# A deformable convolution beside a recurrence: partial sums in a PSUM bank, turned tiles and states in another, tile by tile

## The chip, the cores and the metric

The kernel runs on one core of a Trainium2 chip. The metric is the device time of one execution in microseconds (us). The kernel before took 3271.92 us, the median of three runs (3266.55 to 3273.73).

A core has a tensor engine (PE in the profile; PEld is its loading of weights), a vector engine (VectorE, DVE), a scalar engine (ScalarE, ACT), GpSimd (POOL) and a queue engine for transfers (SyncE, SP). SBUF is the working memory, and PSUM the memory that PE writes its results to. The kernel uses PSUM as eight banks of 128 partitions by 512 fp32 numbers.

## What is computed

The input is `x`, 4 images of 256 channels and 64 by 64 places, all in fp32. There are two layers. Cut to what matters:

```
# layer 0
x = x + deformable_conv(norm_over_channels(x))   # 9 taps, each sampled at 4 corners
t = tokens(x)
t = t + lstm(norm_over_channels(t))              # recurrence over the tokens
# layer 1
x = x + gate(x) * norm_over_channels(x)          # a gate per image and channel, from mean, max, std
t = tokens(x)
t = t + lstm(norm_over_channels(t))
```

The deformable convolution first computes, for each place and tap, an offset and a mask from the normalized input. The sample of a tap is `mask` times the bilinear mean of four corners, `w0*c0 + w1*c1 + w2*c2 + w3*c3`, each corner a vector of 256 channels. The sum over taps of samples times a 256x256 matrix is the output:

```
val = (1-wy)*(1-wx)*corner(y0,x0) + (1-wy)*wx*corner(y0,x1)
    + wy*(1-wx)*corner(y1,x0) + wy*wx*corner(y1,x1)
out = einsum('bkhwc,ock->bohw', val * mask, w_conv)
```

The step of the recurrence has three weighted gates with inputs `x @ U + h @ V + b`, and its cell is not the usual one, `c_new = h * c + i * g`, `h_new = o * tanh(c_new)`.

## The kernel before

**Tiles.** The 16384 places are 128 tiles of 128 places by 256 channels (`NTILE` is 128, `P` 128, `C` 256). A tile holds the same column position of all images, and one time step of the recurrence works on one tile. The order of tiles (`ORDER`) has 16 warm-up tiles ahead of the 128, so that there are 144 steps (`STEPS`).

**Stages.** `prepare` computes offsets and weights and writes the normalized input to a table in DRAM. `sample_and_recur` samples, convolves and runs the first recurrence side by side. `Gate` collects and then forms the gate of the second layer, and `gated_lstm` runs the second recurrence. The change touches `sample_and_recur` and the helper class `Spare`.

**Rounds.** Two units (a tile and a tap) make a round; there are 576 (`PAIRS`). For a round `n`, `gather` (L621) has POOL fetch four corners for each unit into `squares`; `scale` (L642) has ScalarE write `v = w0 * c0`; `combine` (L649) has VectorE add the other three corners with scalar_tensor_tensor, q outer and the two units inner; `turn` (L655) has PE transpose the two `v` into a PSUM bank `tr`; `copy` (L662) has ScalarE bring it to SBUF as `vt`; `convolve` (L669) has PE multiply it with the tap's matrix and add in `acc`. When a pair of tiles has all nine taps, `sampled` (L737) adds the input (`plus`, L711), stores the pair, and asks for the sums of squares (`spread`, L716), which ask for the norms (`norms`, L750, in the parts `begin`, `second`, `last`).

**The path to the recurrence.** `normed` (L832) has ScalarE write normalized tiles `xn`, two at a time; `turned` (L843) has PE make four transposes of them into one PSUM bank, `xt`; `kept` (L854) has ScalarE copy the bank to SBUF as `cm`. `project_part` (L937) multiplies a tile of `cm` with the input weights into the gates' banks `ga` and `gb`, `recur` (L497) adds the state's part, and `core` (L982) places these and the gates at fixed slots: a step is 4.5 slots (`step_slot`, L920), and a slot is a round while there are samples.

**The path from the recurrence.** `added` (L960) has PE transpose a step's state `h` into a PSUM bank `ht`, and VectorE adds it to the tile (`add` inside it, with `plus`). The tile's second norm follows, and then `styled` (L860): ScalarE writes the tile normalized and squared as `y`, VectorE adds it to `lanes` and takes the maximum into `gmx` (`lanes`, `highest`). These feed the gate of the second layer.

**Spare time.** What has no fixed slot is given to `Spare` (L548) for an engine, with a slot from which it may go, an estimate in microseconds and a condition (`room`), such as a free buffer. At each slot, `fill` (L1042) runs what fits in the estimate of the slot's remaining time, from the front of the engine's list; `urgent` puts an item at the front, everything else goes to the end.

**The order of instructions.** All engines run their instructions in the order in which the program gives them (`Ordered`, `InOrder`), one slot after the other: ACT's part, then VectorE's, PE's, and the gathers. The waits between engines follow from which tiles an instruction reads and writes.

**PSUM.** The eight banks are `tr` (2), `acc` (2), `ga`, `gb`, and two of the pool `misc`, with the tags `ms` and `ys`. In `sample_and_recur`, `ht` uses `ms` and `xt` uses `ys`. After the sampling the gate's sums (`Gate.add`, tile `pq`) take `ys`, and `Gate.gates` takes `ms`.

Of the kernel before, what the change touches and what calls it, by code (L numbers as in the profile page):

```python
# [11 lines left out]
F32 = mybir.dt.float32  # L12
I32 = mybir.dt.int32
AF = mybir.ActivationFunctionType
ALU = mybir.AluOpType
# [4 lines left out]
P = 128  # L20
B, C, H, W = 4, 256, 64, 64
T = H * W
NC = C // P
# [13 lines left out]
NB = 8  # L37
# [510 lines left out]
class Spare:  # L548
# [3 lines left out]
    def __init__(self):  # L552
        self.todo = {}

    def give(self, engine, slot, us, do, room=lambda: True, urgent=False):
        left = self.todo.setdefault(engine, [])
        left.insert(0 if urgent else len(left), (slot, us, do, room))

    def run(self, engine, slot, us, late=6):
        left = self.todo.get(engine, [])  # L560
        n = 0
        while n < len(left):
            ready, cost, do, room = left[n]
            if ready <= slot and room() and (cost <= us + 0.3 or slot - ready > late):
                del left[n]
                us -= cost
                do(slot)
                n = 0
            else:
                n += 1  # L570
# [5 lines left out]
def sample_and_recur(  # L576
# [12 lines left out]
    nc = Ordered(tc.nc, pools["after"])  # L589
    ident = const[0]  # L590
# [8 lines left out]
    give = spare.give  # L599
# [5 lines left out]
    LAST = STEPS - NB  # L605
# [36 lines left out]
    def scale(n):  # L642
        r = rounds[n]
        for i in range(2):
            v = vp.tile([P, C], F32, name="v", tag="v", bufs=6)
            nc.scalar.activation(v, r["sq"][i][:, 0:C], AF.Copy, scale=r["w"][i][0])
            r["v"].append(v)

    def combine(n):  # L649
        r = rounds[n]  # L650
        for q in range(1, 4):
            for v, sq, w in zip(r["v"], r["sq"], r["w"]):
                nc.vector.scalar_tensor_tensor(v, sq[:, q * C : (q + 1) * C], w[q], v, ALU.mult, ALU.add)

    def turn(n):  # L655
        r = rounds[n]
# [59 lines left out]
    def spread(n, k, b, j, slot):  # L716

        su, nm, ss = stat(b)
        nc.scalar.activation(nm[:, j : j + k], su[:, j : j + k], AF.Copy, scale=-1.0 / C)
        for i in range(k):  # L720
            c = slice(j + i, j + i + 1)
            sq = sm.tile([P, C], F32, name="sq", tag="sqb", bufs=1)
            nc.scalar.activation(sq, place(n + i)[:, 0], AF.Square, bias=nm[:, c], accum_out=ss[:, c])

        left[b].update(range(j, j + k))
        if b < NTILE // NB:
            parts = (0, NB // 2, 2 * NB if b >= 4 else NB)
        else:
            parts = range(NB, 2 * NB + 1, {STEPS // NB + 1: 2, STEPS // NB: 4}.get(b, NB))
        for lo, hi in zip(parts, parts[1:]):  # L730
            if j in range(lo, hi) and left[b] >= {*range(lo, hi)}:
                norms(b, lo, hi, slot + (2 if LAST <= n < STEPS - 1 else 1))

    left = {b: set() for b in range(STEPS // NB + 2)}
    factors = {}

    def sampled(p, slot):  # L737
        x, a = place(2 * p, 2), acc.pop(p)
        b, j = divmod(2 * p, NB)
        for i in range(2):  # L740
            plus(x[:, i], a[:, i], b, j + i)
        nc.sync.dma_start(x1[:, ORDER[2 * p] : ORDER[2 * p] + 2], x)
        give("ACT", slot + 1, 1.5, lambda s: spread(2 * p, 2, b, j, s))

    eps = sm.tile([P, 2 * NB], F32, name="epsb", tag="epsb", bufs=1)
    nc.vector.memset(eps[:, 0:NB], 1e-5)
# [3 lines left out]
    def norms(b, lo, hi, slot):  # L750


        _, nm, ss = stat(b)
        if b not in factors:
            keep = ("rs", "low") if b < WARM // NB else ()
            factors[b] = [
                sm.tile(
                    [P, 2 * NB], F32, name=n, tag=f"{n}b{b}" if n in keep else f"{n}b", bufs=1 if n in keep else 3
                )
                for n in ("d", "v", "rs", "low")  # L760
            ]
        d, v, rs, low = (f[:, lo:hi] for f in factors[b])
        if hi > NB:
            first = max(lo - NB, 0)
            mine = slice(ORDER[(b - 2) * NB] + first, ORDER[(b - 2) * NB] + hi - NB)
        if lo >= NB:
            rs, low = gate.rs[:, mine], gate.low[:, mine]

        def newton():
            nc.vector.tensor_mul(d, rs, rs)  # L770
            nc.vector.scalar_tensor_tensor(d, d, -0.5, v, ALU.mult, ALU.mult)
            nc.vector.scalar_tensor_tensor(rs, d, 1.5, rs, ALU.add, ALU.mult)

        def begin(slot):
            nc.vector.scalar_tensor_tensor(v, ss[:, lo:hi], 1.0 / C, eps[:, lo:hi], ALU.mult, ALU.add)
            nc.vector.tensor_scalar(
                rs.bitcast(I32), v.bitcast(I32), -0.5, float(0x5F3759DF), ALU.mult, ALU.add
            )
            newton()
            if n0 >= LAST:  # L780
                second(slot)
            else:
                give("DVE", slot, 0.9, second)

        def second(slot):
            newton()
            newton()
            if n0 >= LAST:
                last(slot)
            else:  # L790
                give("DVE", slot, 0.4, last)

        def last(slot):
            nc.vector.tensor_mul(low, nm[:, lo:hi], rs)
            if b < WARM // NB:
                normal[b] = factors[b][2:]
            if lo < NB:
                for p in range(max(lo, FIRST if b == 0 else 0) // 2, min(hi, NB) // 2):
                    give(
                        "ACT",  # L800
                        slot + 1 + 7 * (p - lo // 2),
                        0.9,
                        lambda s, p=p: normed(b, p, *factors[b][2:], s),
                        room("xn", 2),
                    )
            if hi > NB:
                if lo < NB:
                    nc.vector.tensor_copy(gate.rs[:, mine], rs[:, NB + first - lo :])
                    nc.vector.tensor_copy(gate.low[:, mine], low[:, NB + first - lo :])
                if n0 == STEPS - 2:  # L810
                    ending(slot)
                    return
                for p in range(first // 2, (hi - NB) // 2):
                    give(
                        "ACT",
                        slot + 2 + 3 * (p - first // 2),
                        1.15,
                        lambda s, p=p: styled(b - 2, p, s),
                        room("y", 2),
                    )  # L820

        n0 = (b - 2) * NB + lo - NB
        give("DVE", slot, 0.9 if n0 < LAST else 2.2, begin, urgent=n0 >= LAST)


    now, free = {"slot": 0}, [*range(SQUARES)]
    taken = {"xn": 0, "y": 0, "ms": 0, "ys": 0, "cm": 0}

    def room(tag, n):
        return lambda: free if tag == "y" and now["slot"] > PAIRS + 16 else taken[tag] < n  # L830

    def normed(b, p, rs, low, slot):  # L832

        taken["xn"] += 1
        xn = yp.tile([P, 2, C], F32, name="xn", tag="xn")
        n = b * NB + 2 * p
        for i in range(2):
            normalize(nc, xn[:, i], place(n + i)[:, 0], rs, low, 2 * p + i)
        if n < WARM:
            through.update((n, n + 1))  # L840
        give("PE", slot + 1, 0.44, lambda s: turned(n, xn, s), room("ys", 1))

    def turned(n, xn, slot):  # L843
        taken["ys"] += 1
        pt = ps_ms.tile([P, 2, NC, P], F32, name="xt", tag="ys")
        for i in range(2):
            for k in range(NC):
                nc.tensor.transpose(pt[:, i, k], xn[:, i, k * P : (k + 1) * P], ident)
        taken["xn"] -= 1
        give("ACT", slot + 1, 0.6, lambda s: kept(n, pt), room("cm", 6))  # L850

    cms = {}

    def kept(n, pt):  # L854
        taken["cm"] += 1
        cms[n] = cm_p.tile([P, 2, NC, P], F32, name="cm", tag="cm")
        nc.scalar.copy(cms[n], pt)
        taken["ys"] -= 1

    def styled(b, p, slot):  # L860

# [98 lines left out]
    def added(n, slot):  # L960

        h = state.pop(("h", n))
        taken["ms"] += 1
        ht = ps_ms.tile([P, C], F32, name="ht", tag="ms")
        for k in range(NC):
            nc.tensor.transpose(ht[:, k * P : (k + 1) * P], h[:, k], ident)

        def add(slot):
            b, j = divmod(n, NB)
            plus(place(n)[:, 0], ht, b + 2, NB + j)  # L970
            taken["ms"] -= 1
            if j == NB - 1:
                t0 = ORDER[n] - NB + 1
                nc.sync.dma_start(x2[:, t0 : t0 + NB], place(b * NB, NB))
            if n >= LAST:
                spread(n, 1, b + 2, NB + j, slot)
            else:
                give("ACT", slot + 1, 0.9, lambda s: spread(n, 1, b + 2, NB + j, s))

        give("DVE", slot + 1, 0.48, add, urgent=n >= LAST)  # L980
# [79 lines left out]
    s = 0  # L1060
# [865 lines left out]
```

## Time and profile before

| what | value |
|---|---|
| median of three runs | 3271.92 us |
| lowest and highest | 3266.55 and 3273.73 us |
| span of the profiled execution | 3304.8 us |
| first and last gather issued (POOL) | 192.5 and 2304.0 us |
| samples beside the recurrence, full | about 420 to 2300 us |
| first recurrence alone | about 2320 to 2480 us |
| gate and second recurrence | about 2480 to 3305 us |
| sample additions (`v<-squares,used,v`, VectorE) | 3456 of 128x256, mean 477 ns |
| transposes of tiles (`xt`, PE) | 328, copied by 82 of 128x512 (mean 579 ns) |
| transposes of states (`ht`, PE) | 272, read by 128 additions of 128x256 (mean 414 ns) |

Times in the profile are those of one execution, recorded by the hardware; it was some 1% longer than the median of the runs. An instruction's duration runs from its start to its end. Successive instructions of VectorE can overlap, so that the busy time of a group (a union) is less than count times mean. Nearly all instructions carry the line L425, that of the helper that records the order, so that rows are told apart by the names of the tiles: `out<-in`. In group rows, the numbers are: instructions, busy time, mean duration, idle time of the engine just ahead of them, and what ended that idle time. In rows by stage, after the stretch and its length come the busy times of PE, PEld, DVE, ACT and POOL with instruction counts, then the granted clock of PE as a share, the share of DMA engines busy, and GB/s. Timeline rows have a start, a length, and the instructions merged in it; in brackets is the engine's idle time before them and who ended it.

### The profile page before, as it was taken

The page shows a single profiled execution, that of the slowest core. Times are in us where ns is not written, and L with a number is a line of the kernel's source. Part 1 is how long each engine was busy: PE and PEld are TensorE (multiplying, and loading weights), DVE is VectorE, ACT ScalarE, POOL GpSimd, SP SyncE. Part 2 cuts the span into 40 slices and gives each one's busy share as a digit, 9 for nine tenths or more (in the row PEclk, how much of TensorE's full clock was granted, in tenths as well). Part 3 has the DMA queues.
Part 4 walks back from the last instruction along what each step waited for, and adds up shares of the span by engine and source line. Part 5 has one row for each costly group of instructions (what it writes and reads, how often), then busy time and mean ns, then how long its engine had stood idle before and what let it go on. Part 6 is the DMA issues. An engine that isn't in the chain of part 4 may idle for free.

```text
span 3304.8 us, 61570 instructions
## 1 busy us (share of the span) xinstructions
PE 3072.2 (93%) x20428; PEld 2841.5 (86%) x20428; DVE 2621.7 (79%) x7465; ACT 2059.5 (62%) x5450; POOL 1629.7 (49%) x1595
## 2 busy tenths in 40 slices
PE   7957799999999999999999999999896999999998
PEld 6945688898899989898888888989894999999997
DVE  6666677888898988898889888979567777777774
ACT  6724455566666666676666666757775666666663
POOL 3366666665566666675757656656000022222221
PEclk9978899999999999999999999999997999999999
DMA  9988787898989989888889988888101044444442
GB/s 314 326 292 322 292 280 285 297 321 300 329 298 336 326 295 333 308 310 312 301 309 328 317 295 309 312 311 304 62 14 71 26 138 153 148 151 153 147 141 85
DMA packets 311432, 822.38 MB, mean 249 GB/s; under 512 B 100024, under 2 KB 105528, under 8 KB 306496
## 3 DMA queue, kind: packets, MB, share of 16 engines
q0 software_dynamic: 189312, 672.57, 58.6%
q1 hardware_dynamic: 121360, 145.15, 12.9%
q8 instruction: 164, 2.69, 0.3%
q14 instruction: 164, 1.34, 0.1%
q10 hardware_dynamic: 432, 0.63, 0.1%
HBM read 698.32 MB, written 119.89 MB: 248 GB/s over the span
## 4 chain that ended last, share of the span: by engine, by line
PE 84%; ACT 5%; DVE 3%; issue 3%; another core or an unknown queue 2%; DMA 2%; POOL 0%; SPq 0%; ACTq 0%; DVEq 0%; POOLq 0%
PE acc L425 28%; PE ga L425 14%; PE gacc L425 7%; PE gtr L425 7%; PE tr L425 7%; PE gb L425 7%; PE ggb L425 4%; PE gga L425 4%; ACT v L425 1%; PE xt L425 1%; PE zacc L425 1%; DMA squares<-table,used 1%; PE ht L425 1%; DMA table<-ring 1%
## 5 line engine op out<-in xcount | busy, mean ns | idle before, releaser
L425 POOL DMA_INDIRECT squares<-table,used x1152 | 1376.3, 1195 | 743.7 <-issue 167.8
L425 DVE SCALAR_TENSOR_TENSOR v<-squares,used,v 128x256 f32<-128x256 f32 x3456 | 1412.8, 477 | 163.0 <-ACT v L425 110.1
L425 PE MATMUL acc<-wconv,vt 128*128 128x256 f32 x4608 | 1132.4, 390 | 105.9 <-ACT vt L425 70.5
L425 PEld LDWEIGHTS acc<-wconv,vt 128*128 128x128 f32 x4608 | 854.2, 196 | 216.7 <-ACT vt L425 78.7
L425 ACT COPY vt<-tr 128x512 f32<-128x512 f32 x576 | 336.1, 584 | 727.4 <-PE tr L425 514.5
L425 ACT ACTIVATE v<-squares,used 128x256 f32<-128x256 f32 x1152 | 529.1, 512 | 72.2 <-DMA squares<-table,used 63.3
L425 PE MATMUL tr<-ident,v 128*128 128x128 f32 x2304 | 351.5, 275 | 29.2 <-DVE v L425 24.9
L425 PEld LDWEIGHTS tr<-ident,v 128*128 128x128 f32 x2304 | 276.4, 142 | 43.9 <-DVE v L425 23.0
L425 PEld LDWEIGHTS ga<-cm,Us 128*128 128x128 f32 x2272 | 274.8, 192 | 24.4 <-ACT cm L425 15.3
L425 DVE TENSOR_TENSOR tg<-tg,ti 128x256 f32<-128x256 f32 x284 | 119.8, 422 | 220.7 <-ACT ti L425 193.7
L425 PE MATMUL ga<-cm,Us 128*128 128x128 f32 x2272 | 279.2, 276 | 13.6 <-ACT cm L425 10.9
L425 PEld LDWEIGHTS ga<-h,Vs 128*128 128x128 f32 x2256 | 275.3, 193 | 7.3 <-issue 0.3
L425 PE MATMUL ga<-h,Vs 128*128 128x128 f32 x2256 | 276.8, 276 | 0.1
L425 POOL DMA_DIRECT2D hd<-sqh x60 | 34.9, 581 | 395.5 <-DVE sqh L425 359.2
L425 POOL DMA_DIRECT2D ring<-hd x240 | 144.5, 630 | 165.6 <-DMA hd<-sqh 156.8
L425 DVE TENSOR_TENSOR h<-to,th 128x256 f32<-128x256 f32 x282 | 119.0, 422 | 126.6 <-ACT th L425 113.0
L425 ACT ACTIVATE tg<-gacc,bs 128x128 f32<-128x128 f32 x284 | 89.0, 364 | 176.7 <-PE gacc L425 176.7
L425 PEld LDWEIGHTS gb<-cm,Us 128*128 128x128 f32 x1136 | 148.4, 192 | 12.2 <-issue 4.4
L425 PE MATMUL gb<-cm,Us 128*128 128x128 f32 x1136 | 152.1, 275 | 4.6 <-issue 3.4
L425 PEld LDWEIGHTS gacc<-h,Vs 128*128 128x128 f32 x1128 | 146.0, 191 | 10.1 <-DVE h L425 3.2
L425 PEld LDWEIGHTS gb<-h,Vs 128*128 128x128 f32 x1128 | 146.4, 192 | 7.8 <-issue 1.8
L425 PE MATMUL gb<-h,Vs 128*128 128x128 f32 x1128 | 149.5, 275 | 2.2 <-issue 2.2
(226 smaller groups left out, 4575.6 us busy)
## 6 DMA issues: line engine op xcount, KB each, us to landing
squares<-table,used POOLq DMA_INDIRECT x1152
ring<-in_x_dram SPq DMA_DIRECT2D x65, 256.0 KB
x1d<-ring SPq DMA_DIRECT2D x64, 256.0 KB
x2d<-ring SPq DMA_DIRECT2D x16, 1024.0 KB
ring<-x2d SPq DMA_DIRECT2D x16, 1024.0 KB
out_dram<-ring SPq DMA_DIRECT2D x32, 512.0 KB
hd<-sqh POOLq DMA_DIRECT2D x60, 256.0 KB
ring<-hd POOLq DMA_DIRECT2D x240, 64.0 KB
```

The source lines that it names most:

```text
L425: ins = op(*args, **kw)
```

## The change

Nothing of the arithmetic's result is changed. Three things are different.

First, `combine` writes the first two of the three additions of a sample to `partial`, a PSUM tile of two halves (one for each unit of the round) that takes the bank `ys` and is allocated once. The first addition reads `v` (SBUF) and writes `partial`, the second reads and writes `partial`, the third reads `partial` and writes `v`.

Second, `xt` and `ht` share the bank `ms`: the tile `turns`, allocated once, has a half for each. As half a bank holds one tile, `turned` makes two transposes of one tile instead of four of a pair, `kept` copies one tile into its half of `cm`, and the second tile of the pair follows when the first has been copied. The count `xt` (of one) stands where `ys` was.

Third, `give` has a new flag `soon`: an item with it goes behind the urgent and soon items that are in the list and ahead of all others. It is set for the sums of squares of sampled tiles, the three parts of their norms (`lo < NB`), `normed`, `turned` and `kept`.

```
-    def give(self, engine, slot, us, do, room=lambda: True, urgent=False):
+    def give(self, engine, slot, us, do, room=lambda: True, urgent=False, soon=False):
         left = self.todo.setdefault(engine, [])
-        left.insert(0 if urgent else len(left), (slot, us, do, room))
+        at = 0 if urgent else sum(t[4] for t in left) if soon else len(left)
+        left.insert(at, (slot, us, do, room, urgent or soon))
...
+    partial = ps_ms.tile([P, 2, C], F32, name="partial", tag="ys")
+    turns = ps_ms.tile([P, 2, C], F32, name="turns", tag="ms")
+
     def combine(n):
         r = rounds[n]
         for q in range(1, 4):
-            for v, sq, w in zip(r["v"], r["sq"], r["w"]):
-                nc.vector.scalar_tensor_tensor(v, sq[:, q * C : (q + 1) * C], w[q], v, ALU.mult, ALU.add)
+            for i, (v, sq, w) in enumerate(zip(r["v"], r["sq"], r["w"])):
+                nc.vector.scalar_tensor_tensor(
+                    v if q == 3 else partial[:, i],
+                    sq[:, q * C : (q + 1) * C],
+                    w[q],
+                    v if q == 1 else partial[:, i],
+                    ALU.mult,
+                    ALU.add,
+                )
...
-        give("ACT", slot + 1, 1.5, lambda s: spread(2 * p, 2, b, j, s))
+        give("ACT", slot + 1, 1.5, lambda s: spread(2 * p, 2, b, j, s), soon=True)
...
-        give("PE", slot + 1, 0.44, lambda s: turned(n, xn, s), room("ys", 1))
-
-    def turned(n, xn, slot):
-        taken["ys"] += 1
-        pt = ps_ms.tile([P, 2, NC, P], F32, name="xt", tag="ys")
-        for i in range(2):
-            for k in range(NC):
-                nc.tensor.transpose(pt[:, i, k], xn[:, i, k * P : (k + 1) * P], ident)
-        taken["xn"] -= 1
-        give("ACT", slot + 1, 0.6, lambda s: kept(n, pt), room("cm", 6))
+        give("PE", slot + 1, 0.22, lambda s: turned(n, xn, 0, s), room("xt", 1), soon=True)
+
+    def turned(n, xn, i, slot):
+        taken["xt"] += 1
+        pt = turns[:, 0].rearrange("p (k q) -> p k q", k=NC)
+        for k in range(NC):
+            nc.tensor.transpose(pt[:, k], xn[:, i, k * P : (k + 1) * P], ident)
+        give("ACT", slot + 1, 0.35, lambda s: kept(n, pt, i), room("cm", 6) if i == 0 else lambda: True, soon=True)
+        if i == 0:
+            give("PE", slot + 2, 0.22, lambda s: turned(n, xn, 1, s), room("xt", 1), soon=True)
+        else:
+            taken["xn"] -= 1
...
-        cms[n] = cm_p.tile([P, 2, NC, P], F32, name="cm", tag="cm")
-        nc.scalar.copy(cms[n], pt)
-        taken["ys"] -= 1
+    def kept(n, pt, i):
+        if i == 0:
+            taken["cm"] += 1
+            halves[n] = cm_p.tile([P, 2, NC, P], F32, name="cm", tag="cm")
+        nc.scalar.copy(halves[n][:, i], pt)
+        taken["xt"] -= 1
+        if i == 1:
+            cms[n] = halves.pop(n)
...
-        ht = ps_ms.tile([P, C], F32, name="ht", tag="ms")
+        ht = turns[:, 1]
```

`begin`, `second` and `last` are given with `soon=lo < NB`, and `normed` with `soon=True`.

More of the change, by code (lines that the diff above doesn't have):

```diff
@@ L562, in run @@
         while n < len(left):
-            ready, cost, do, room = left[n]
+            ready, cost, do, room, _ = left[n]
             if ready <= slot and room() and (cost <= us + 0.3 or slot - ready > late):
@@ L782, in begin @@
             else:
-                give("DVE", slot, 0.9, second)
+                give("DVE", slot, 0.9, second, soon=lo < NB)
         def second(slot):
@@ L790, in second @@
             else:
-                give("DVE", slot, 0.4, last)
+                give("DVE", slot, 0.4, last, soon=lo < NB)
         def last(slot):
@@ L804, in last @@
                         room("xn", 2),
+                        soon=True,
                     )
@@ L822, in norms @@
         n0 = (b - 2) * NB + lo - NB
-        give("DVE", slot, 0.9 if n0 < LAST else 2.2, begin, urgent=n0 >= LAST)
+        give("DVE", slot, 0.9 if n0 < LAST else 2.2, begin, urgent=n0 >= LAST, soon=lo < NB)
     now, free = {"slot": 0}, [*range(SQUARES)]
-    taken = {"xn": 0, "y": 0, "ms": 0, "ys": 0, "cm": 0}
+    taken = {"xn": 0, "y": 0, "ms": 0, "xt": 0, "cm": 0}
     def room(tag, n):
@@ L840, in normed @@
             through.update((n, n + 1))
-        give("PE", slot + 1, 0.44, lambda s: turned(n, xn, s), room("ys", 1))
-    def turned(n, xn, slot):
-        taken["ys"] += 1
-        pt = ps_ms.tile([P, 2, NC, P], F32, name="xt", tag="ys")
-        for i in range(2):
-            for k in range(NC):
-                nc.tensor.transpose(pt[:, i, k], xn[:, i, k * P : (k + 1) * P], ident)
-        taken["xn"] -= 1
-        give("ACT", slot + 1, 0.6, lambda s: kept(n, pt), room("cm", 6))
-    cms = {}
-    def kept(n, pt):
-        taken["cm"] += 1
-        cms[n] = cm_p.tile([P, 2, NC, P], F32, name="cm", tag="cm")
-        nc.scalar.copy(cms[n], pt)
-        taken["ys"] -= 1
+        give("PE", slot + 1, 0.22, lambda s: turned(n, xn, 0, s), room("xt", 1), soon=True)
[9 more added lines that the diff above has]
+            taken["xn"] -= 1
+    cms, halves = {}, {}
+    def kept(n, pt, i):
[6 more added lines that the diff above has]
+            cms[n] = halves.pop(n)
     def styled(b, p, slot):
```

## The prediction

> **What bounds the kernel now.** I read the header of the page, then the busy time of each engine by stage, the chain of waits inside the long stage, the groups of that stage, and single instructions in the timeline.
>
> ```profile
> span 3304.8 us, 61570 instructions
> PE 3072.2 (93%) x20428; PEld 2841.5 (86%) x20428; DVE 2621.7 (79%) x7465; ACT 2059.5 (62%) x5450; POOL 1629.7 (49%) x1595
> ```
>
> The profiled execution took 3304.8 us, 32.9 above the median of the runs (3271.9). My sum is a difference against the profile, and I carry it over to the median. Busy time by stage, in the order PE, PEld, DVE, ACT, POOL:
>
> ```profile
> 420.00:2300.00 1880.00, 1802.69 (x12037) 1672.68 (x12036) 1615.22 (x4409) 1222.61 (x3266) 1217.49 (x1022) 0.99 0.88 310
> 2320.00:2480.00 160.00, 147.10 (x1261) 143.77 (x1259) 93.99 (x272) 116.83 (x342) 0.00 (x0) 0.99 0.11 39
> ```
>
> The first row is the stage in which samples are gathered and convolved while the first recurrence runs: PE 96%, VectorE 86%. PE has 4097 `acc` matmul records there, 8 to a round, so 512 rounds at 3.67 us. Nine rounds hold two time steps, so a step takes 16.5 us and the stage holds 114 of them. The second row is the rest of the first recurrence, without samples. The chain of waits (1200 to 1240 us):
>
> ```profile
> by line: PE acc L425 43.9%; PE ga L425 20.4%; PE tr L425 11.9%; PE gb L425 8.9%; another core or an unknown queue 4.4%; ACT sq L425 3.0%; ACT v L425 2.3%; ACT vt L425 1.6%; issue 1.5%; PE ht L425 1.1%; PE xt L425 1.1%; ACT nm L425 0.3%
> ```
>
> PE is the bound, but not by much. From the pieces of that chain: `tr` 0.44 and `acc` 1.73 us a round; `ga` 1.78 twice, `gb` 0.89 twice, `ht` 0.22 and half an `xt` (0.22) a step. That is 4.5 x 2.17 + 5.34 + 0.44 = 15.55 us of PE per step, 0.95 (5.8%, 108 us in the stage) below the period. VectorE's own work per step, start to start: 27 sample instructions of 0.396 (10.69); four for the state, 0.459 twice and 0.343 twice (1.60); two residual adds of 0.34 (0.68); half of `lanes` 1.136 and of `gmx` 0.602 (0.87); small norms about 0.5. Together 14.3 us. So **VectorE has 2.2 us of slack per step**, and that slack decides this case.
>
> **Part 1: the partial sums.** A round has six scalar_tensor_tensor (STT): three weights, two samples alternating. They now add in `v`; after the change the first and second additions write halves 0 and 1 of one PSUM bank, `partial`, and the second and third read them there. No instruction is added. The question is the price of one. VectorE's timeline:
>
> ```profile
> 1206.31 0.41 DVE L425 SCALAR_TENSOR_TENSOR ring<-ring,ht 128x256 f32<-128x256 f32 x1
> 1206.65 0.08 DVE L425 DVE_READ_ACCUMULATOR ring<-ring,ht 128x1 f32 x1
> 1206.65 2.50 DVE L425 SCALAR_TENSOR_TENSOR v<-squares,used,v 128x256 f32<-128x256 f32 x6
> ...
> 1212.68 0.43 DVE L425 TENSOR_TENSOR tg<-tg,ti 128x256 f32<-128x256 f32 x1
> 1213.14 0.43 DVE L425 TENSOR_TENSOR cell<-hc,tg 128x256 f32<-128x256 f32 x1
> ```
>
> Six sample STTs take 2.50 us: each lasts 472 ns, but the next starts 396 ns after it, because each depends on the one before the last and neighbours overlap by some 76 ns. An STT with a PSUM input (`ring<-ring,ht`) lasts 414 and lets the next start after 340. `tg` and `cell` show the other case: `cell` needs `tg`, there is no overlap, and it starts 34 ns after `tg`'s end. A second row bears on the pointer weight:
>
> ```profile
> 2488.00 0.74 DVE L425 TENSOR_SCALAR squares<-ring,grs,glow 128x256 f32<-128x256 f32 x2
> ```
>
> Two pointer scalars and one SBUF tensor: two of them in 0.74 us, 0.33 apart. Pointers cost nothing there; the dear form is two SBUF tensors with a pointer. So for the four STTs per round that read `partial` I take the `ht` row, 414 long and 340 apart; for the two that read `v` (two SBUF inputs as now) 472 and 396. Writes into PSUM by VectorE are in no row; I take them at the price of SBUF writes and keep 0 to 60 ns for the range.
>
> [...] Overlapping writes of VectorE do wait for one another in this program, though the engine runs in order; here each row overwrites the same scratch:
>
> ```profile
> 2501.69 1.01 DVE L425 TENSOR_SCALAR_CACHE_REDUCE squares<-squares,u 128x768 f32<-128x768 f32 x1 [4.07 <-DMA squares<-ud]
> 2502.63 0.08 DVE L425 DVE_READ_ACCUMULATOR squares<-squares,u 128x1 f32 x1
> 2502.75 1.01 DVE L425 TENSOR_SCALAR_CACHE_REDUCE squares<-squares,u 128x768 f32<-128x768 f32 x1
> ```
>
> The second begins 36 ns after the whole end of the first. No tile of this kernel is written by VectorE in PSUM, so the trace can't show whether halves of a bank are kept apart. The two sums:
>
> By address: two at 396 and four at 340, 2.15 us a round against 2.38: -1.0 us a step, VectorE 13.3. By bank: two at 472 + 34 and four at 414 + 34, 2.80 us a round: +1.9 us a step, VectorE 16.3; if all six stay 472 long, 3.04 us a round and 17.3.
>
> [...] VectorE then has 16.3 us of work in a step that takes 16.5 and becomes the bound. No bound here runs without loss: PE loses 5.8% now, to late `vt` copies (PE waits 34 us for `vt` in the stage) and to waits of ACT that the profile gives to no engine (146 us). VectorE moreover waits for `ti` and `th` at fixed places in its order (98 us). With 5% lost a step takes 17.1 us: +0.6 x 114 = 70 us. The 17.3 end, with the same loss, is +1.7 x 114 = 190 us; the low end, VectorE's losses swallowed by waits it has anyway, is 0. Nearer to the low row I take **+80 us**. Queued behind a slower VectorE: the `tr` transposes (PE), the `vt` copy and next `v` scaling (ACT), and the gathers on POOL, five rounds ahead and with POOL 65% busy; ACT waits only 8.3 us for gathered squares in the stage, so that cover holds.
>
> **Part 2: the shared bank.** `xt` and `ht` had a bank each; now half a bank each. `xt` comes one tile at a time: two transposes, a copy of 128x256, again. PE issues the same matmuls. ACT copies 2 x 437 ns (between the 128x128 activation from PSUM, 364, and the 128x512 copy, 584) instead of 584: +0.29 x 71 = 21 us on an engine 65% busy in the stage; cost 0, and the 21 us if ACT were late. By bank, PE's transposes of `xt` also wait until VectorE has read `ht`, the reverse too, and ACT's copy waits for VectorE's read. PE runs only about 1 us behind VectorE, and behind a stuck transpose stand the `tr` of the round and the gates. Before, transposes waited 4 us for `ht`'s reader and 14 us for `xt`'s in the whole run. Twice as many pairs of users: **+15 us**, between 0 and 40.
>
> **Part 3: first in spare time.** The turned tiles' norms, copies and transposes go ahead of the second layer's statistics (`y`, `lanes`, `gmx`) and of the residual adds. Where this helps is just behind the samples:
>
> ```profile
> 2359.66 1.12 PE L425 MATMUL xt<-ident,xn 128*128 128x128 f32 x4 [4.87 <-ACT cm L425]
> ```
>
> PE stands 4.87 us because ACT does `y` work (2.09 us a piece) ahead of the `cm` copy that frees the bank. Between 2320 and 2480 PE idles 12.9 us, 10.0 of them in front of `xt`. I take **-10 us**, between -13 and 0. What is late next is the same `y` work, given back when samples are over: one tile pair a step fits there (ACT 73% busy), cost 0, and 2.3 us for each pair left over. The SP queue keeps its transfers in their order. The second recurrence (2480 to the end, 825 us) isn't touched.
>
> **Sum.** +80 + 15 - 10 = +85: 3304.8 + 85 = 3390 for a profiled run, 3271.9 + 85 = 3357; I say **3355 us**, slower. Its own range is 3285 (VectorE's waits swallowed, sharing +15) to 3450 (17.3 us a step).
>
> **Rivals.** *Halves kept apart by address.* [...] PE's own 15.55 us then bound: of the 108 us lost a quarter goes (those that start with a late `v`), -27, sharing +5 without bank waits, the spare order -10: about 3240 us, from 3205 to 3264. It decides as soon as STTs of a round start under 396 ns apart. *PE caught in the shared bank.* VectorE unhurt, but `xt` and `ht` wait in each other's readers once a step: 114 x 0.5 us = +57, order -10, VectorE -10: 3310, from 3280 to 3340. Against it: the transposes waited so little before. *Nothing arrives.* PE bound as before, gains and waits cancel: 3272. That the change doesn't do what it says is excluded for parts 2 and 3 (they are plain orders); for part 1 it is the first case.
>
> **Chances.** By bank 0.60, by address 0.22, shared bank 0.12, nothing 0.06. What a measurement of this kernel can tell from no change is about 0.2%, 6.5 us. Faster: 0.22 and the lowest end of the first case, 0.24. Same: 0.05. Slower: 0.71. Range 3235 to 3435: it leaves out the better half of the second case (0.1) and the top of the first (0.08).
>
> **What would show it.** Right: six STTs take about 2.8 us or more instead of 2.50, no overlap, their starts over 440 ns apart; VectorE over 93% in the stage, PE under 93%; PE's waits for VectorE's `v` grow; no 4.87 us gap before `xt` at the end. Wrong: STTs into `partial` that overlap (starts 340 to 396 apart) would turn the sign; an STT that writes PSUM at well over 472 ns would take it above the range.

## The result and the profile after

The changed kernel took 3386.05 us (3382.96 to 3390.2), the kernel before 3272.82 us (four runs, 3266.55 to 3283.41): ratio 1.0349, 95% interval 1.0304 to 1.0394, 113 us more. Of the profiled execution:

```profile
span 3381.1 us, 62309 instructions
PE 3078.7 (91%) x20428; PEld 2823.2 (83%) x20428; DVE 2833.5 (84%) x7465; ACT 2075.3 (61%) x5521; POOL 1406.3 (42%) x1595
```

The span is 76 us longer than that of before; the difference of the medians is larger because the profiled execution of before was itself 33 us above its median. VectorE has the same 7465 instructions and 212 us more of busy time; PE's busy time is the same. By stage (length, then PE, PEld, DVE, ACT, POOL), with the samples, and behind them:

```profile
420.00:2300.00 1880.00, 1734.56 (x11499) 1590.71 (x11499) 1719.22 (x4217) 1180.58 (x3169) 980.60 (x979) 0.99 0.88 297
...
2392.00:2560.00 168.00, 151.12 (x1265) 148.09 (x1264) 100.14 (x287) 120.95 (x363) 0.00 (x0) 0.96 0.10 37
```

In the same 1880 us PE does 4% less and VectorE is busy 91% instead of 86%. The samples end at 2392 us, 74 us later than before; the rest of the first recurrence takes 167 us (before 165) and what follows 821 us in both. So nearly the whole loss lies in the stage with the samples. From the 100th to the 500th round, by the first addition of each, a round takes 3.66 us before and 3.86 after; 0.197 us more in each of 576 rounds is 113 us, the loss of the medians. The additions there, in VectorE's timeline:

```profile
1201.40 1.06 DVE L425 SCALAR_TENSOR_TENSOR partial<-squares,used,v 128x256 f32<-128x256 f32 x2
1202.50 1.01 DVE L425 SCALAR_TENSOR_TENSOR partial<-squares,used,partial 128x256 f32<-128x256 f32 x2
1203.62 0.87 DVE L425 SCALAR_TENSOR_TENSOR v<-squares,used,partial 128x256 f32<-128x256 f32 x2
1204.58 1.08 DVE L425 SCALAR_TENSOR_TENSOR partial<-squares,used,v 128x256 f32<-128x256 f32 x2
```

One round took 2.50 us before and takes 3.0 to 3.2 now. A pair that writes `partial` lasts 1.01 or more, two full durations and a gap; the last pair, which only reads it, 0.87, and overlaps as before. Start to start, the medians are 583, 528, 525, 594 and 398 ns, and 392 or 564 to what follows; before, all were 396. The durations, from the groups (instructions, busy time, mean ns, idle time in front):

```profile
L425 DVE SCALAR_TENSOR_TENSOR partial<-squares,used,v 128x256 f32<-128x256 f32 x1152 | 568.1, 493 | 85.4 <-ACT v L425 17.4
L425 DVE SCALAR_TENSOR_TENSOR partial<-squares,used,partial 128x256 f32<-128x256 f32 x1152 | 564.4, 490 | 40.4
L425 DVE SCALAR_TENSOR_TENSOR v<-squares,used,partial 128x256 f32<-128x256 f32 x1152 | 502.1, 477 | 62.8 <-DVE partial L425 2.3
```

The duration grew little, from 477 to 493, 490 and 477. What went is the overlap of 76 ns, and gaps came in its place: 35 ns where an addition waits only for its neighbour, 91 and 104 where it waits for something else as well. Who VectorE waits for, in total us, times and longest, before:

```profile
DVE tg L425 <- ACT ti L425: 77.4, 48, 8.1
DVE v L425 <- ACT v L425: 56.6, 35, 5.4
```

and after (the longest row of all, and the one for `v`):

```profile
DVE v L425 <- DVE partial L425: 2.3, 5, 0.5
...
DVE partial L425 <- ACT v L425: 0.4, 1, 0.4
```

In the stage it waited 198 us for something other than itself before, and 2 us after: VectorE is now the bound, and nearly all its idle time is the short gaps behind its own instructions (144 of 161 us stand in front of the sample additions).

### The profile page after: what moved, and what is told of

It is laid out like the page before. It is cut to its first block, busy times and chain, and to the rows that moved or that the text cites. A ratio compares the mean times of both kernels' runs of the same rounds, so it can differ in the third digit from the quotient of the medians.

```text
span 3381.1 us, 62309 instructions
## 1 busy us (share of the span) xinstructions
PE 3078.7 (91%) x20428; PEld 2823.2 (83%) x20428; DVE 2833.5 (84%) x7465; ACT 2075.3 (61%) x5521; POOL 1406.3 (42%) x1595
## 5 line engine op out<-in xcount | busy, mean ns | idle before, releaser
L425 POOL DMA_INDIRECT squares<-table,used x1152 | 1153.1, 1001 | 1035.9 <-DVE v L425 221.7
L425 PE MATMUL acc<-wconv,vt 128*128 128x256 f32 x4608 | 1107.3, 384 | 12.4 <-ACT vt L425 12.0
L425 PEld LDWEIGHTS acc<-wconv,vt 128*128 128x128 f32 x4608 | 840.7, 192 | 106.8 <-ACT vt L425 13.0
L425 DVE SCALAR_TENSOR_TENSOR partial<-squares,used,v 128x256 f32<-128x256 f32 x1152 | 568.1, 493 | 85.4 <-ACT v L425 17.4
L425 DVE SCALAR_TENSOR_TENSOR partial<-squares,used,partial 128x256 f32<-128x256 f32 x1152 | 564.4, 490 | 40.4
L425 DVE SCALAR_TENSOR_TENSOR v<-squares,used,partial 128x256 f32<-128x256 f32 x1152 | 502.1, 477 | 62.8 <-DVE partial L425 2.3
L425 PE MATMUL tr<-ident,v 128*128 128x128 f32 x2304 | 360.4, 277 | 74.3 <-DVE v L425 68.6
L425 PEld LDWEIGHTS tr<-ident,v 128*128 128x128 f32 x2304 | 266.7, 142 | 117.8 <-issue 80.9
L425 ACT ACTIVATE th<-cell 128x256 f32<-128x256 f32 x256 | 106.7, 417 | 202.3 <-DVE cell L425 151.1
```

Of the source, the lines that this page charges most:

```text
L425: ins = op(*args, **kw)
```

## The experiments

They ran on three chips: the first four on one, "The shared bank where VectorE bounds" on another, the rest on a third. The kernel before took 3161 to 3164 us on each of them, some 110 us less than in the main measurement, whose chip is not on record. Ratios are to runs of before made beside the experiment, with 95% intervals.

**All sums in SBUF.** The change without its first part.

```
-    partial = ps_ms.tile([P, 2, C], F32, name="partial", tag="ys")
...
-                nc.vector.scalar_tensor_tensor(
-                    v if q == 3 else partial[:, i],
...
+                nc.vector.scalar_tensor_tensor(v, sq[:, q * C : (q + 1) * C], w[q], v, ALU.mult, ALU.add)
```

> The changed kernel with the additions back in v (SBUF); the shared bank and the spare order stay. Theory A (VectorE's six additions wait for one another because both halves of the bank count as one object): the six start 396 ns apart again, VectorE has slack again, a round takes about 3.65 us, total 3260 to 3280 us. Theory C (PE stuck in the bank that xt and ht share is what costs): still 3340 to 3385 us. Theory B (a PSUM operand is dearer in itself): as A here.

Measured: 3174.66 us, ratio 1.0039 (1.0025 to 1.0053). As Theory A has it, nearly all of the loss is gone (205 us, against the changed kernel's 3379.89 beside the experiments, below), though the bank of `turns` is still shared. The absolute numbers in the first four expectations rest on the 3272 us of the main measurement. The starts are 396 ns apart again:

```profile
1203.01 2.46 DVE L425 SCALAR_TENSOR_TENSOR v<-squares,used,v 128x256 f32<-128x256 f32 x6
```

**One unit in PSUM.** The first unit adds in `partial[:, 0]`, the second in `v`.

```
-                    v if q == 3 else partial[:, i],
+                    v if q == 3 or i == 1 else partial[:, 0],
...
-                    v if q == 1 else partial[:, i],
+                    v if q == 1 or i == 1 else partial[:, 0],
```

> The changed kernel with only the first unit of a round adding in the PSUM bank, the second in v. Neighbouring additions no longer touch the same bank. A: starts 396 to 415 ns apart and a total within 15 us of the kernel with all sums in SBUF (3260 to 3290). B (PSUM operands dear in themselves): half of the loss remains, about 3325 us. If reading PSUM saved time, as the row of the residual addition suggested to me (340 ns to the next start), the total falls below the kernel with sums in SBUF.

Measured: 3165.34 us, 1.0008 (0.9998 to 1.0018). A's first clause holds, and the overlap is back with PSUM operands (one round):

```profile
1203.77 0.55 DVE L425 SCALAR_TENSOR_TENSOR partial<-squares,used,v 128x256 f32<-128x256 f32 x1
1204.23 0.47 DVE L425 SCALAR_TENSOR_TENSOR v<-squares,used,v 128x256 f32<-128x256 f32 x1
1204.63 0.48 DVE L425 SCALAR_TENSOR_TENSOR partial<-squares,used,partial 128x256 f32<-128x256 f32 x1
1205.02 0.47 DVE L425 SCALAR_TENSOR_TENSOR v<-squares,used,v 128x256 f32<-128x256 f32 x1
1205.41 0.47 DVE L425 SCALAR_TENSOR_TENSOR v<-squares,used,partial 128x256 f32<-128x256 f32 x1
1205.81 0.47 DVE L425 SCALAR_TENSOR_TENSOR v<-squares,used,v 128x256 f32<-128x256 f32 x1
```

From the second addition of the round on, neighbours start 392 to 397 ns apart whichever memory they use (the first, behind a residual addition, lasts 0.55 us, and the second starts 0.46 us after it). So a PSUM operand is neither dear (Theory B falls) nor the 56 ns cheaper that I had read from the residual addition. The total is nonetheless below that with all sums in SBUF, by 9 us; the section on the hardware returns to it.

**Waits without PSUM.** The kernel before with its two loops exchanged.

```
-        for q in range(1, 4):
-            for v, sq, w in zip(r["v"], r["sq"], r["w"]):
+        for v, sq, w in zip(r["v"], r["sq"], r["w"]):
+            for q in range(1, 4):
```

> The kernel before with the two loops of the additions exchanged: all three additions of a unit in a row, in SBUF. Waits without PSUM. A: four of six additions wait for their neighbour, start 472 + 34 = 506 ns apart instead of 396, 2.82 us a round against 2.38, VectorE at 16.3 us a step near the period of 16.5: 3285 to 3330 us. B: as before, 3273 us.

Measured: 3282.19 us, 1.0378 (1.0363 to 1.0393). The same six instructions in SBUF, only in another order:

```profile
1203.82 2.96 DVE L425 SCALAR_TENSOR_TENSOR v<-squares,used,v 128x256 f32<-128x256 f32 x6
```

The waits alone cost 120 us: an addition behind its predecessor starts 515 or 521 ns after it (479 or 485 long, then 36). That answers B, under which nothing should have changed. The cost is more than the 12 to 57 us expected, which were reckoned from a step of 16.5 us; in the profile of before nearest to the experiments (below) a round takes 3.48 us, 15.6 a step, and VectorE has less slack.

**The spare order alone.** Before with `soon`, set at the same places.

```
-        give("PE", slot + 1, 0.44, lambda s: turned(n, xn, s), room("ys", 1))
+        give("PE", slot + 1, 0.44, lambda s: turned(n, xn, s), room("ys", 1), soon=True)
...
-        give("ACT", slot + 1, 0.6, lambda s: kept(n, pt), room("cm", 6))
+        give("ACT", slot + 1, 0.6, lambda s: kept(n, pt), room("cm", 6), soon=True)
```

> The kernel before with nothing but the spare order (the flag soon); xt and ht keep a bank each and four transposes at a time. A: the gap of 4.9 us in front of xt behind the samples goes, 8 to 13 us less than before, 3260 to 3265 us. If the spare order only moves work: 3273 us; if the statistics of the second layer end up behind the last step: over 3280 us.

Measured: 3152.22 us, 0.9966 (0.9955 to 0.9978). The size is as expected, 10 us, but not the place. Behind the samples PE still stands in front of `xt`, as long as before:

```profile
2205.43 1.11 PE L425 MATMUL xt<-ident,xn 128*128 128x128 f32 x4 [4.56 <-ACT cm L425]
```

The gain lies among the samples. The profile without the flag that comes nearest is that of before without two operations of VectorE (below; on another chip, with before's time). There PE waits in the stage for one thing:

```profile
PE ga L425 <- ACT cm L425: 10.4, 10, 1.0
```

With the flag no wait of PE is listed there, and the samples end at 2162 us instead of 2182. The rest of the recurrence takes 170 us against 167.

**The changed kernel on this chip.** No edit.

> The changed kernel itself, beside the runs of before on this chip: before took 3163 us on the chip of the first experiments and 3273 us on that of the change. If VectorE's chain of additions bounds the changed kernel (A), its time hardly moves with the chip, 3360 to 3386 us, and the ratio is 1.06 to 1.07 where before takes 3163. If the loss is a fixed part of the time that before takes: ratio 1.035.

Measured: 3379.89 us, 1.0679 (1.0665 to 1.0693). Before is 108 us faster here than in the main measurement, the changed kernel 6 us: what bounds it is not what slowed before there.

**A bank each again, one tile at a time.** As with all sums in SBUF, and `xt` takes the bank `ys`.

```
+    singles = ps_ms.tile([P, C], F32, name="singles", tag="ys")
...
-        pt = turns[:, 0].rearrange("p (k q) -> p k q", k=NC)
+        pt = singles.rearrange("p (k q) -> p k q", k=NC)
```

> As the kernel with sums in SBUF (spare order, one tile at a time), but xt has the bank that the partial sums had, and ht keeps the other. If the 22 us between the kernel with sums in SBUF (3174.7) and that with the spare order alone (3152.2) come from users of one bank waiting for one another: ratio to before 0.996 to 1.000 as with the spare order alone. If they come from turning one tile at a time: 1.003 to 1.005 again.

Measured: 3156.19 us, 0.9963 (0.9949 to 0.9977). Turning one tile at a time costs nothing that shows. Sharing the bank costs the difference to 3174.66 us, 18 us. The two ran on different chips (before took 3164 and 3163 us beside them), but the same shows in the profiles, shared bank first, then a bank each:

```profile
420.00:2150.00 1730.00, 1718.04 (x11686) 1608.13 (x11685) 1562.98 (x4280) 1193.02 (x3231) 1172.56 (x995) 1.00 0.93 329
```

```profile
420.00:2150.00 1730.00, 1730.00 (x11802) 1623.65 (x11801) 1579.11 (x4326) 1207.01 (x3263) 1179.61 (x1004) 1.00 0.93 332
```

With a bank each PE is never idle in the stretch and gets 1% more matmuls done. From the 100th to the 500th round, a round takes 3.487 us with the shared bank (and as much with one unit in PSUM), 3.451 without.

**Less for VectorE, changed and before.** While samples run, the additions to `lanes` and the maxima in `gmx` are left out.

```
-        nc.vector.tensor_add(gate.lanes, gate.lanes, y)
+        if slot > PAIRS:
+            nc.vector.tensor_add(gate.lanes, gate.lanes, y)
...
-        nc.vector.tensor_max(gate.mx, gate.mx, y[:, 0])
+        if now["slot"] > PAIRS:
+            nc.vector.tensor_max(gate.mx, gate.mx, y[:, 0])
```

> The changed kernel without two operations of VectorE while samples run: the sums and maxima of y for the second layer's gate (lanes and gmx, 0.87 us a step) are left out there, so the gate's numbers are those of the last steps alone. A (VectorE bounds): about 0.87 us less a step, in some 100 steps, 75 to 100 us less than the changed kernel. C (PE's waits in the shared bank bound): less than 20 us.

> The same left out of the kernel before (the gate's sums and maxima while samples run). There VectorE has 2 us of slack a step: no more than 10 us less than before.

Measured: changed 3318.05 us, 1.0482 (1.0467 to 1.0497), 62 us less than the changed kernel; before 3164.76 us, 0.9997 (0.9988 to 1.0006), no change. The 62 us fall short of the 75 expected: some 44 pairs of 1.74 us were taken out, 76 us. But the contrast settles which engine bounds: the same work is free before and is four fifths of its length after. By stage in the changed kernel with less:

```profile
420.00:2300.00 1880.00, 1776.10 (x11853) 1637.94 (x11852) 1709.12 (x4273) 1221.74 (x3276) 985.50 (x1011) 0.99 0.89 307
```

VectorE is as full as in the profile after (91%), and PE gets 3% more matmuls done in the same time (11853 against 11499).

**The shared bank where VectorE bounds.** Loops exchanged, sums in SBUF, and parts 2 and 3 of the change.

> The kernel before with the additions of a unit in a row (as units_outer, sums in SBUF), and in addition the shared bank and the spare order of the change. What the shared bank costs where VectorE is the bound: units_outer took 1.0378 of before. If PE's waits in that bank count in full there too (22 us of the bank, less 10 for the order): 1.041 to 1.043. If they fall into PE's slack: 1.034 to 1.038.

Measured: 3262.60 us, 1.0321 (1.0303 to 1.0339), below the case without them (1.0378; another chip) and below both expected ranges. PE's waits in the bank are there (in total us, times):

```profile
  PE turns L425: 74.4, 67
  PEld turns L425: 62.6, 47
```

but they don't reach VectorE: from 420 to 2150 us it waits for no other engine here, against 16 us in the kernel with the exchanged loops alone. So the shared bank costs nothing that shows, and the two parts together save some 18 to 20 us, more than the order alone did where PE bounds. What the order alone would save here was not run.

**Less spare work per slot behind the samples.** The spare order alone, with a limit for ScalarE in the twelve slots from `PAIRS + 4`; and the spare order alone once more.

```
-            spare.run(engine, s, 9.0)
+            spare.run(engine, s, 2.2 if engine == "ACT" and s < PAIRS + 16 else 9.0)
```

> The kernel with the spare order alone (0.9966 of before), and in the twelve slots behind the samples ScalarE gets at most 2.2 us of spare work a slot instead of 9.0, so that the cm copy that PE waits for isn't behind a heap of y. My prediction put the gain of the spare order there; the gap of 4.6 us in front of xt stayed. If that heap is what PE waits for: 4 to 9 us below the spare order alone, 0.994 to 0.995. If y is only put off to steps that have no room for it: 0.997 or more.

> The same with 3.4 us a slot. Between the spare order alone (0.9966) and the limit of 2.2 us.

> The spare order alone once more, beside these two: 0.995 to 0.998 of before.

Measured: 3147.01 us, 0.9962 (0.9949 to 0.9975) with 2.2 us; 3149.70 us, 0.9968 (0.9957 to 0.998) with 3.4; 3155.19 us, 0.9975 (0.9965 to 0.9986) with the order alone. The profiles show 165, 165 and 171 us between the samples and the end of the first recurrence, and with 2.2 us the longest wait of `xt` for `cm` there falls from 4.44 to 1.57 us, so the limit does what it should there. The median with 2.2 us is 8 us below that of the order alone, as much as expected, but the ratios miss the expected 0.994 to 0.995 and their intervals overlap: the further gain is not shown. What does hold is that the spare order alone is faster than before and than the changed kernel: 0.9966 and 0.9975 in two measurements.

## Why the prediction was right, step by step

**The sign and the mechanism** were right. The halves of the bank count as one object in this program, VectorE's additions wait for one another, and VectorE takes over from PE as the bound. Shown by the starts (from 396 to 525 ns and more), by the exchanged loops (waits alone, in SBUF, cost 120 us), and by the work that is free before (no change in time) and not after (62 us).

Of the signs named in advance two did not come: VectorE is busy 91% of the stage, not over 93, because the gaps of 35 to 104 ns count as idle, and PE still stands up to 3.6 us in front of a turned tile behind the samples.

That the sum goes by bank (the two halves as one object), with its 2.80 us a round, was my assumption: VectorE writes no tile in PSUM before, so no run of before shows that term. In its place the runs of the changed kernel show 3.02 to 3.19 us a round, and starts of 525 to 594 ns behind an addition that writes the bank, which bear the assumption out. It is the program that waits, VectorE for itself (`DVE v <- DVE partial` in the list after): the chip was not asked to run halves of a bank without these waits. That they come from the bank is read from the two units that overlap as soon as one of them leaves it (392 to 397 ns from start to start), and from the last pair, which only reads the two halves and overlaps (398 ns). Being parts of one tile is not enough: the prediction's row at 2488.00 has two instructions that write neighbouring parts of the SBUF tile `squares`, 0.33 us apart. Two separate tiles in one bank were not run, so that a PSUM tile and its bank are not told apart.

**The size** was 83 us forecast against 113 measured, 3355 against 3386, inside the range. The term that was mis-sized is the round in part 1: I took 2.80 us, with 3.04 as the far end, and it is 3.02 to 3.19. Two things were wrong in it. I priced an addition that reads `partial` at 414 ns, by the residual addition, whose scale is a constant; the ones here, with a pointer for the weight, take 477 to 490. And I gave each wait 34 ns, while two a round, with a second thing to wait for, take 91 and 104. In the other direction, the 5% that I added for a bound's losses was too much: VectorE's work is 14.3 + 4.5 x 0.64 = 17.2 us a step, and a step takes 17.3 (489 rounds in the 1880 us, 3.84 each), under 1% more. The step itself was forecast at 17.1: an error of 0.9 us in the work and one of 0.7 in the losses cancelled, and that the sum came within 31 us is luck to this extent.

**The starting point.** The 113 us hold only against the 3273 us of before in the main measurement. Beside the experiments before took 3164 us and the same change cost 216. What the mechanism fixes is the time of the changed kernel, 3386 and 3380 us; the 16.5 us a step, from which I took the difference, were partly stalls that before did not have there (last section).

**Part 2**, +15 us: 18 us where PE bounds, nothing that shows where VectorE does; in the profile after, VectorE waited 2 us in all for others. So in the sum, which had VectorE as the bound, it should have been 0; I added two costs of which only one can count at a time.

**Part 3**, -10 us: where PE bounds the size was right (7 to 10), the place wrong; what it gives in the changed kernel itself was not measured. I read one gap of 4.87 us behind the samples and gave the order the credit for it; the gap stayed, because in those slots ScalarE may do everything that is ready, `y` too (with ScalarE limited there, it fell from 4.44 to 1.57 us). The gain is in the samples, where PE waited for `cm` ten times in the nearest profile without the flag.

**The rivals.** "By address" would have shown starts under 396 ns, and the changed kernel doesn't; had it come true, its price would have been wrong too, as with a PSUM operand the starts are 392 to 397 ns apart against 396, which saves VectorE 4 ns at most, not 56. "PE caught in the shared bank" exists, at 18 us rather than 57, and only while PE is the bound.

## What to carry to other kernels

Before two streams of one engine are put into halves of one PSUM tile in a bank, look at whether they overlap now: if their rows last longer than the time from start to start, the overlap is what can be lost. Here the starts went from 396 ns apart to 525 and more behind every addition that writes the bank. Take the price of an instruction from a row with the same operands, scalars included, and not from one that shares only the memory. When a change makes another engine the bound, the waits that it brings to the old one can stop costing (18 us here where PE bounded, nothing that showed where VectorE did), and the sum must not hold both. The time that rested on the new bound carried over to another measurement (3386 and 3380 us); the difference to the old kernel (113 and 216 us) did not, because the old kernel's time (3273 and 3164 us) did not.

## What the hardware showed that was not expected

**Gathers got faster.** POOL's gather instructions (count, busy time, mean ns, idle), before, after, with one unit in PSUM, and with the loops exchanged, one row from each kernel:

```profile
L425 POOL DMA_INDIRECT squares<-table,used x1152 | 1376.3, 1195 | 743.7 <-issue 167.8
```

```profile
L425 POOL DMA_INDIRECT squares<-table,used x1152 | 1153.1, 1001 | 1035.9 <-DVE v L425 221.7
```

```profile
L425 POOL DMA_INDIRECT squares<-table,used x1152 | 1205.8, 1047 | 760.9 <-DVE v L425 181.9
```

```profile
L425 POOL DMA_INDIRECT squares<-table,used x1152 | 1141.1, 991 | 949.8 <-DVE v L425 376.6
```

They drop from 1195 (1146 to 1183 beside the experiments, with all sums in SBUF and the loops as before) to about 1000 ns both with a PSUM input and with mere gaps between VectorE's instructions, and to 1047 when a third of the additions (unit 0's second and third) have one input in SBUF, without gaps. With one unit in PSUM the starts are as close together as with all sums in SBUF, so the PSUM operands are what differs there. The exchanged loops have two inputs in SBUF throughout and drop as far (991 ns), so the inputs are not the whole of it. What makes the gathers faster was not shown, and times on POOL are rough in these profiles. Whether this is worth anything to the time is open. The kernel with one unit in PSUM is 9 us faster than that with all sums in SBUF, but their profiles differ only before the 100th round (in rounds 40 to 100, 3.30 us a round against 3.42). Both values occur with slow gathers too: 3.31 and 3.30 with the spare order alone, 3.42 with the limit of 3.4 us.

**Before stalls in the main measurement.** Before took 3273 us there and 3161 to 3164 on three chips later, the changed kernel 3386 and 3380. The profile of before from the main measurement has stretches in which PE, VectorE and ScalarE stand still together; one of them:

```profile
1501.23 0.42 DVE L425 SCALAR_TENSOR_TENSOR ring<-ring,ht 128x256 f32<-128x256 f32 x1 [4.24 <-remote]
1501.32 0.59 ACT L425 COPY vt<-tr 128x512 f32<-128x512 f32 x1 [5.97 <-remote]
1501.96 2.50 PE L425 MATMUL acc<-wconv,vt 128*128 128x256 f32 x5 [5.51 <-ACT vt L425]
```

(`remote`: the profile gives the end of the wait to no engine of the core.) Between 420 and 2300 us there are 33 of them of over 0.3 us, 43 us in all; PE is idle for 77 us, against 10 in 1730 us in the later profile of before without two operations of VectorE. The later profiles hold just one, of 0.3 us, and the changed kernel has none in the main measurement either. So VectorE's chain does not hide these stalls: they are absent, and what causes them, the chip or the circumstances, is open. The same change is 3.5% slower in the one measurement and 6.8% in the other.
